# Sorting the tokens of three batches by expert: 48 dense expert tiles become 19 gathered ones

## The chip, the cores and the metric

The kernel runs on one core of one Trainium2 chip, in one launch; the other cores do nothing. The metric is the device time of one execution in microseconds (us). Engines are named as in the profile: PE (TensorE, with PEld for its weight loads), DVE (VectorE), ACT (ScalarE), POOL (GpSimd) and SP (SyncE, which here mostly issues DMAs). A letter q behind an engine's name means the sequencer of that engine, with waits and DMA issues.

## The reference, cut to what matters

A decoder of two layers works on x of 4 batches x 256 tokens x 256 features, all in float32. Layer 0 has self-attention, attention over a memory of 4 x 1601 x 256, and a quantised feed-forward. Layer 1 has a recurrence, a cross attention (16 query heads of 128 features, 4 key/value heads, 256 + 1601 = 1857 keys, taken in 15 chunks of 128), and then, last, a mixture of eight experts of which each token uses two:

```python
xf = layernorm(x).reshape(-1, 256)                # 1024 tokens
top_logits, top_idx = top_k(xf @ w_gate, 2)       # 8 experts
weights = softmax(top_logits)
# for each token, over its two experts e:
h0, h1 = xf @ wi_0[e], xf @ wi_1[e]               # 256 -> 128 each
y = (silu(h0) * h1) @ wo[e]                       # 128 -> 256
out = x + sum over the two of weight * y
```

The reference sorts the 2048 (token, expert) pairs by expert and multiplies each group by its expert's weights; any way that gives the same sum will do.

## The kernel before, in words

One function, `decoder_kernel`, holds the program. Its parts are Python generators: each `yield` ends a piece, and the order in which pieces are called is the order in which work reaches the scheduler. The scheduler fixes the order on every engine when the kernel is built; on the chip each engine then works through its own list strictly in order, and waits at an instruction until its inputs and buffers are ready. SP issues nearly all DMAs, also in order.

In the first part four generators `before(b)`, one for each batch, run staggered up to the recurrence of layer 1. In the second part `steps()` walks through the cross attention. Its unit is a `Pair`: one batch, one key/value head and two query heads (b, g, h), 32 pairs in all, each with eight steps of two key chunks. A pair's number is in its tile names (`sum320` is the sum of pair b=3, g=2, h=0). For each step

- `score` multiplies keys by queries (L1361, tile `bsc`); ACT copies the scores out into an `s` tile of a ring of twelve (L1362), DVE keeps a running maximum (L1364, L1366),
- `exponential` follows ten steps later: DVE subtracts the maximum (L1383), ACT takes the exponential (L1386), POOL adds the two chunks to the pair's `sum` (L1389, L1398),
- `weigh` follows eleven steps later: the `s` tiles times the values (L1407, tile `bpo`); `finish` turns the sum (L1421), and multiplies by the output weights (L1437, tile `bpw`), which DVE adds to `x` (L1441).

Each step has two places, 2s and 2s+1, at which `others(place)` runs small pieces of other work. `put(place, gen, last, bank)` books them: the keys and queries of the next head (`prep_kv`, `prep_q`, with their rotation on DVE and POOL and the product `pk` at L1290), the pieces of `maximum` and `finish`, and the experts of batches 0, 1 and 2, which can start when their batch's attention is over.

`experts(b)` is dense: all eight experts are worked out for all 256 tokens, and the gates are zero where a token did not choose the expert. It normalises x (`mo`), multiplies by the gate weights (`pl`), finds the two largest of eight by comparisons on DVE, and then for each expert

- `inner(e)`: four matmuls of 128x256 into `mph` (L1053), one tanh on ACT (L1058), two DVE operations of 128x256 (L1059, L1060);
- `outer(e, it)`: two matmuls of 128x256 into `mpe` (L1066), two DVE operations x += gate * y (L1071).

Three batches x eight experts x two halves of the tokens are 48 expert tiles of 128 rows. The pieces of batches 0 and 1 are all placed between attention steps; of batch 2 the last six pieces (`KEPT = 3`, two at a time) are left until the last attention is over, where they run with the first pieces of `experts(3)`. After that `experts(3)` ends the kernel.

Of the kernel before, what the change touches and what calls it, by code (L numbers as in the profile page):

```python
# [10 lines left out]
F32 = mybir.dt.float32  # L11
I32 = mybir.dt.int32
# [3 lines left out]
AF = mybir.ActivationFunctionType  # L16
ALU = mybir.AluOpType
AX = mybir.AxisListType
# [16 lines left out]
TERN = 34  # L35
SIDE = 48
KEPT = 3
KEYS = (3,)
EARLY = tuple((b, i) for b in range(3) for i in range(4))
LATE = tuple((3, i) for i in range(4))  # L40
# [4 lines left out]
RATE = 1  # L45
START = (0, 3, 8, 13)
NE, ME = 8, 128
NEG = -1.0e30
SCALE1 = float(np.float32(1.0) / np.sqrt(HD1).astype(np.float32))
QCLIP = 128.0 - 1e-6  # L50
# [6 lines left out]
def _constants():  # L57
    f = np.float32
    p = np.arange(P)
    c = {}  # L60
    c["ident"] = np.eye(P, dtype=f)

    c["tri"] = np.where(p[None, :] <= p[:, None], 0.0, NEG).astype(f)

    c["par"] = (p[:, None] // HD0 % 2 == np.arange(2)[None, :]).astype(f)

    def interleaved(ang):
        cos, sin = np.cos(ang.astype(np.float64)), np.sin(ang.astype(np.float64))
        return np.repeat(cos, 2, 1), np.stack([-sin, sin], -1).reshape(len(ang), -1)

    def halves(ang):
        cos, sin = np.cos(ang.astype(np.float64)), np.sin(ang.astype(np.float64))
        return np.concatenate([cos, cos], 1), np.concatenate([-sin, sin], 1)

    t = np.arange(S, dtype=f)[:, None]
    freq0 = (np.arange(0, HD0, 2, dtype=f) / f(HD0)) * np.log(f(30000.0))
    freq1 = f(1.0) / f(10000.0) ** (np.arange(0, 16, 2, dtype=f) / f(16))
    for n, (cc, ss) in (("r0", interleaved(t * freq0[None])), ("r1", halves(t * freq1[None]))):
        for m, a in (("c", cc), ("s", ss)):
            c[n + m] = a.astype(f).reshape(2, P, 16).transpose(1, 0, 2).reshape(P, 32)  # L80
    c["ones"] = np.ones((P, P), f)
    freq2 = 1.0 / 10000.0 ** (np.arange(0, HD1, 2) / HD1)
    c["invf"] = np.broadcast_to(freq2.astype(f)[None], (P, 64))
    ch = p // 32
    same = ch[:, None] == ch[None, :]
    c["cum"] = (same & (p[:, None] <= p[None, :])).astype(f)
    c["first"] = (same & (p[:, None] % 32 == 0)).astype(f)
    last = p % 32 == 31
    k8 = np.arange(8)
    selc = [(last[:, None] & (4 * j + ch[:, None] <= k8[None])) for j in range(2)]  # L90
    sell = [(last[:, None] & (4 * j + ch[:, None] == k8[None])) for j in range(2)]
    c["selcum"] = np.stack(selc, 1).astype(f).reshape(P, 16)
    c["sellast"] = np.stack(sell, 1).astype(f).reshape(P, 16)
    c["selstab"] = np.broadcast_to((p == 31)[:, None], (P, 8)).astype(f)
    sx = np.zeros((P, 8), f)
    sx[:8] = k8[:, None] < k8[None]
    c["strict8"] = sx
    ex = np.zeros((P, 2, P), f)
    for j in range(2):
        ex[:8, j] = k8[:, None] == 4 * j + ch[None]  # L100
    c["expand"] = ex.reshape(P, 2 * P)
    c["dmask"] = (p[:, None] % 16 == np.arange(16)[None]).astype(f)
    c["iota8"] = np.broadcast_to((k8 - 8.0)[None], (P, 8)).astype(f)
    at, off = {}, 0
    for n, a in c.items():
        at[n] = (off, a.shape[1])
        off += a.shape[1]
    return np.ascontiguousarray(np.concatenate(list(c.values()), 1), dtype=f), at
# [8 lines left out]
def decoder_kernel(ctx: ExitStack, tc: tile.TileContext, at, t, out):  # L117
# [43 lines left out]
    def fa(b, name, dt=F32):  # L161

        return fr.tile([P, 512], dt, tag=f"a{b}", name=name, bufs=NA)
# [5 lines left out]
    def db(name):  # L169

        return wk.tile([P, 1024], F32, tag="db", name=name, bufs=NDB)

    def sm(shape, tag, name, bufs=2, dt=F32):
        return small.tile(shape, dt, tag=tag, name=name, bufs=bufs)
# [34 lines left out]
    def cc(name):  # L209
        o, n = at[name]  # L210
        return cst[:, o : o + n]
# [83 lines left out]
    def centred(xh, xb, mv, r):  # L295
        xh = xh.rearrange("p (j d) -> p j d", j=2)
        nm = sm([P, 2], "nmr", f"nmr{uid()}", 4)
        V.scalar_tensor_tensor(nm, mv[:, :, 0], -1.0, r[:, 0:2], ALU.mult, ALU.mult)
        for j in range(2):
            A.activation(xh[:, j, :], xb[:, j, :], AF.Identity, bias=nm[:, j : j + 1], scale=r[:, j : j + 1])  # L300
        return xh
# [674 lines left out]
        yield  # L976


    def experts(b):
        xb = xs[b]  # L980

        final = b == B - 1

        def ea(name, place=0):
            return fa(place if final else 2, name)

        wgt = sm([P, 2, NE], "wgt", f"wgt{b}", 1)
        nc.sync.dma_start(out=wgt, in_=t["wgt"].rearrange("(c p) n -> p c n", p=P))
        s8 = [P, 2, NE]
# [3 lines left out]
        r1 = rsqrt(mv[:, :, 1], 1e-5, f"mo{b}")  # L993
        yield
        xh = centred(ea(f"mxh{b}"), xb, mv, r1)
        yield
        tp = to_features(xh, f"mo{b}")
        yT = ea(f"yTm{b}")
# [12 lines left out]
        for k in range(2):  # L1011
            m = sm([P, 2], f"m{k}", f"mm{b}{k}", 1)
            V.tensor_reduce(m, lg, AX.X, ALU.max)
            oh = sm(s8, f"oh{k}", f"oh{b}{k}", 1)
            V.tensor_tensor(oh, lg, m[:, :, None].to_broadcast(s8), ALU.is_equal)
            V.tensor_mul(oh, oh, iota)
            ix = sm([P, 2], "ix", f"ix{b}{k}", 1)
            V.tensor_reduce(ix, oh, AX.X, ALU.min)
            V.tensor_tensor(oh, iota, ix[:, :, None].to_broadcast(s8), ALU.is_equal)
            if k == 0:  # L1020
                V.scalar_tensor_tensor(lg, oh, NEG, lg, ALU.mult, ALU.add)
            tops.append(m)
            hots.append(oh)
# [4 lines left out]
        w1 = sm([P, 2], "w1", f"w1{b}", 1)  # L1028
        V.tensor_scalar(w1, w2, 1.0, None, ALU.add)
        V.reciprocal(w1, w1)  # L1030
        V.tensor_scalar(w1, w1, 0.5, None, ALU.mult)
        V.tensor_mul(w2, w2, w1)
        gts = sm(s8, f"gts{final}", f"gts{b}", 1)
        V.tensor_mul(gts, hots[0], w1[:, :, None].to_broadcast(s8))
        V.tensor_mul(hots[1], hots[1], w2[:, :, None].to_broadcast(s8))
        V.tensor_add(gts, gts, hots[1])
        yield
        weights = {}

        def inner(e):  # L1040
            e2 = e - e % 2
            if e == e2:
                wi = db(f"wi{b}{e2}").rearrange("p (i c n) -> p i c n", i=2, c=2)
                for i, name in enumerate(("wi0", "wi1")):
                    nc.sync.dma_start(
                        out=wi[:, i], in_=t[name][:, e2 * ME : (e2 + 2) * ME].rearrange("(c p) n -> p c n", p=P)
                    )
                weights[e2] = wi, weight(fa(3, f"we{b}{e2}"), "woe", e2 * ME, (e2 + 2) * ME, 0, D)
            wi = weights[e2][0]
            ph = p1(f"mph{b}{e}")  # L1050
            for i in range(2):
                for c in range(2):
                    T.matmul(  # L1053
                        ph[:, i * 256 : i * 256 + 256], lhsT=wi[:, i, c, e % 2 * ME : (e % 2 + 1) * ME], rhs=yT[:, c, :],
                        start=c == 0, stop=c == 1,
                    )
            it = ea(f"it{b}{e}", 1)[:, 0:256]
            A.activation(it, ph[:, 0:256], AF.Tanh, scale=0.5)  # L1058
            V.scalar_tensor_tensor(it, it, 1.0, ph[:, 0:256], ALU.add, ALU.mult)  # L1059
            V.tensor_mul(it, it, ph[:, 256:512])  # L1060
            return it
# [11 lines left out]
                )  # L1073


        ahead = 2 if final else 0
        its = []
        for e in range(NE + ahead):
            if e < NE:
                its.append(inner(e))  # L1080
                if not final:
                    yield
            if e >= ahead:
                outer(e - ahead, its[e - ahead])
            yield
        for j in range(2):
            (nc.scalar if final and j else nc.sync).dma_start(out=out[b, j * P : (j + 1) * P], in_=xb[:, j, :])
        yield

    def before(b):  # L1090
# [15 lines left out]
    def run(gen):  # L1106
        for _ in gen:
            pass
# [351 lines left out]
    def put(place, gen, last=False, bank=False):  # L1460
        while bank and place in taken:
            place += 1
        if bank:
            taken.add(place)
        places.setdefault(place, []).append((gen, last))
        return place
# [46 lines left out]
        gen = loader(b, g)  # L1513
        put(base + 60, gen, True)
    for b in range(B - 1):
        gen = experts(b)
        spot = 2 * (64 * (b + 1) + 17)

        pieces = 23 if b < B - 2 else 23 - 2 * KEPT
        for i in range(pieces):  # L1520
            spot = put(spot, gen, i == 22, i not in (0, 1, 2, 5, 6)) + (5 if i > 6 else 3)
    kept = gen

    def others(place):
        for gen, last in places.pop(place, ()):
# [72 lines left out]
    gen = experts(B - 1)  # L1598
    for _ in range(KEPT):
        next(gen)  # L1600
        next(kept)
        next(kept)
    run(kept)
    run(gen)


# [63 lines left out]
```

## Time and profile before

| what | value |
|---|---|
| median of three runs | 1749.77 us (1748.74 to 1751.0) |
| the profiled execution | 1749.43 us, of which 1747.4 us is the span in the trace |
| mean granted TensorE clock | 0.993 |
| engine with the largest share of the span | PE, 97% |
| end of the last attention matmul (`bpw`, L1437) | 1712.0 us |
| from there to the span's end | 35.4 us |

In the answers of the trace a line of the timeline reads: start in us, busy us, engine, line, operation, output <- inputs, shapes, number of instructions run together, and in brackets the idle time ahead of it and what ended that. A float32 matmul leaves two matmul records, so eight records of `mph` are the four matmuls of one expert. Busy times of a row of matmuls overlap a little; the distance from one start to the next row's start is the time that the work takes of the engine's order. "PEclk" is the clock that the chip granted to TensorE, 1 being full.

### The profile page before, as it was taken

How to read it: one execution, taken by the hardware profiler on the slowest of the kernel's cores; microseconds unless marked ns; L12 is line 12 of the kernel's file. 1: busy time of each engine (PE TensorE's matmuls, PEld its weight loads, DVE VectorE, ACT ScalarE, POOL GpSimd, SP SyncE). 2: the span in 40 equal slices, each digit the busy share in tenths (PEclk: the TensorE clock that was granted, in tenths of full speed). 3: DMA queues.
4: the chain of work that ended last, by engine and by line, in shares of the span. 5: the costliest groups of instructions: out<-in, count | busy, mean ns of one | idle time of the engine just before them, and what ended most of it. 6: DMA issues, size and time to landing. Idle time of an engine off the chain costs nothing.

```text
span 1747.4 us, 20643 instructions
## 1 busy us (share of the span) xinstructions
PE 1694.9 (97%) x6642; PEld 971.5 (56%) x6642; DVE 1302.7 (75%) x2429; ACT 997.4 (57%) x1742; POOL 877.5 (50%) x719
## 2 busy tenths in 40 slices
PE   8899989999999999999999999999999999999998
PEld 4455668765555455554555555555555555445546
DVE  6653476787668777787877878777877878788776
ACT  3456653656456656566665656556565656656551
POOL 2210032211126576676766756655665776676651
PEclk9999999999999999999999999999999999999999
DMA  7221334212231121121212121121222113011102
GB/s 258 99 90 50 90 99 128 75 66 90 97 109 46 38 82 35 55 58 31 89 32 70 47 67 52 55 82 35 73 61 67 51 37 93 26 37 48 43 0 67
DMA packets 113554, 119.10 MB, mean 68 GB/s; under 512 B 10000, under 2 KB 87332, under 8 KB 113448
## 3 DMA queue, kind: packets, MB, share of 16 engines
q1 hardware_dynamic: 111624, 116.39, 21.6%
q10 hardware_dynamic: 1824, 1.41, 0.3%
q8 instruction: 53, 0.87, 0.2%
q14 instruction: 53, 0.43, 0.1%
HBM read 100.20 MB, written 17.57 MB: 67 GB/s over the span
## 4 chain that ended last, share of the span: by engine, by line
PE 64%; DVE 12%; POOL 9%; ACT 9%; issue 4%; DMA 1%; POOLq 0%; DVEq 0%; ACTq 0%
PE bpo L1407 17%; PE bsc L1361 16%; PE pk L1290 5%; POOL sum L1398 5%; PE mph L1053 2%; PE bpw L1437 2%; PE vah L355 2%; ACT s L1386 2%; ACT s L1362 2%; DVE acc L1366 1%; PE xpo L740 1%; DVE s L1383 1%; PE pq L1239 1%; POOL ropeq L1196 1%; PE xsc L695 1%
## 5 line engine op out<-in xcount | busy, mean ns | idle before, releaser
L1398 POOL TENSOR_TENSOR sum<-sum,s 128x512 f32<-128x512 f32 (+1 forms) x411 | 536.7, 1306 | 84.1 <-ACT s L1386 59.0
L1361 PE MATMUL bsc<-qTb,kTb 128*128 128x512 f32 (+1 forms) x960 | 459.5, 599 | 6.8 <-ACT kTb L1303 6.7
L1407 PE MATMUL bpo<-s,vb 128*128 128x512 f32 (+1 forms) x960 | 459.9, 598 | 0.4 <-ACT s L1386 0.4
L1362 ACT ACTIVATE s<-bsc,kn 128x512 f32<-128x512 f32 (+1 forms) x480 | 316.5, 683 | 211.6 <-PE bsc L1361 194.6
L1366 DVE SCALAR_TENSOR_TENSOR acc<-bsc,kn,acc 128x512 f32<-128x512 f32 x448 | 333.0, 743 | 89.2 <-ACT s L1362 73.3
L1383 DVE TENSOR_TENSOR s<-s,bc 128x1024 f32<-128x1024 f32 (+1 forms) x256 | 289.4, 1142 | 14.7 <-PE bc L1379 14.5
L1386 ACT ACTIVATE s<-s 128x1024 f32<-128x1024 f32 (+1 forms) x256 | 256.5, 1006 | 53.8 <-DVE s L1383 52.2
L1361 PEld LDWEIGHTS bsc<-qTb,kTb 128*128 128x128 f32 (+1 forms) x960 | 174.2, 188 | 191.9 <-issue 135.3
L1407 PEld LDWEIGHTS bpo<-s,vb 128*128 128x128 f32 (+1 forms) x960 | 169.8, 191 | 141.7 <-issue 137.9
L1389 POOL TENSOR_TENSOR sum<-s 128x512 f32<-128x512 f32 x32 | 40.8, 1276 | 198.6 <-ACT s L1386 198.6
L1196 POOL TENSOR_TENSOR ropek<-ropek,ropuk 128x512 f32<-128x512 f32 (+1 forms) x64 | 78.2, 1222 | 123.7 <-DVE ropuk L1191 122.4
L1203 ACT ACTIVATE ropeq<-ropeq,rnq 128x128 f32<-128x128 f32 x128 | 41.2, 390 | 110.7 <-POOL rnq L1199 107.1
L355 PE MATMUL vah<-wv,vcT 128*128 128x512 f32 (+1 forms) x156 | 77.7, 633 | 5.1 <-DMA vcT<-in_ctxT 3.1
L1290 PEld LDWEIGHTS pk<-wkv,cTk 128*128 128x128 f32 x624 | 76.3, 192 | 8.3 <-issue 4.5
L1290 PE MATMUL pk<-wkv,cTk 128*128 128x128 f32 x624 | 77.4, 275 | 0.0
L1199 POOL TENSOR_TENSOR kn<-ssk,nhalf 128x4 f32<-128x4 f32 (+1 forms) x64 | 66.2, 1034 | 17.5 <-DVE ssk L1198 15.0
L1364 DVE TENSOR_SCALAR acc<-bsc,kn 128x512 f32<-128x512 f32 x32 | 24.0, 750 | 59.7 <-ACT s L1362 59.7
L1437 PEld LDWEIGHTS bpw<-wo,aT 128*128 128x128 f32 x256 | 48.5, 190 | 34.8 <-issue 21.1
L272 POOL TENSOR_TENSOR rsr_xa<-rse_xa,nhalf 128x2 f32<-128x2 f32 x4 | 3.4, 854 | 126.0 <-DVE rse_xa L270 126.0
L1437 PE MATMUL bpw<-wo,aT 128*128 128x256 f32 x256 | 65.6, 379 | 0.3 <-ACT aT L1413 0.3
L1196 POOL TENSOR_TENSOR ropeq<-ropeq,ropuq 128x512 f32<-128x512 f32 x32 | 43.8, 1368 | 40.2 <-PE bsc L1361 17.8
L358 ACT COPY vst<-vah 128x512 f32<-128x512 f32 (+1 forms) x52 | 30.2, 591 | 56.0 <-issue 18.3
(509 smaller groups left out, 2589.7 us busy)
## 6 DMA issues: line engine op xcount, KB each, us to landing
v<-vst SPq DMA_DIRECT2D x48, 256.0 KB
vb<-v SPq DMA_DIRECT2D x48, 256.0 KB
cTk<-in_ctxT SPq DMA_DIRECT2D x24, 512.0 KB
wq<-in_wq SPq DMA_DIRECT2D x16, 512.0 KB
wo<-in_wo SPq DMA_DIRECT2D x16, 512.0 KB
wi<-in_wi SPq DMA_DIRECT2D x32, 256.0 KB
xcT<-in_ctxT SPq DMA_DIRECT2D x12, 512.0 KB
xct<-in_ctx SPq DMA_DIRECT2D x12, 512.0 KB
```

The costliest lines, as they stand in the source:

```text
L355: T.matmul(pv[0:r, :], lhsT=cT[:, c, k * P : k * P + r], rhs=wv[c], start=c == 0, stop=c == 1)
L1196: G.tensor_tensor(r4, r4, u4[:, :, ::-1, :], ALU.add)
L1199: G.tensor_tensor(rn, ss[:, 0:n], nhalf[:, 0:n], ALU.pow)
L1290: T.matmul(pk[:, q, 0:w], lhsT=src, rhs=e["wkv"][:, c, 0:w], start=c == 0, stop=c == 1)
L1361: T.matmul(pc[0:n, :], lhsT=e["kT"][:, k * P : k * P + n], rhs=q, start=True, stop=True)
L1362: A.activation(s[0:n, i, :], pc[0:n, :], AF.Copy, scale=e["kn"][0:n, k : k + 1])
L1366: V.scalar_tensor_tensor(self.acc[0:n, :], pc[0:n, :], e["kn"][0:n, k : k + 1], self.acc[0:n, :], ALU.mult, ALU.max)
L1383: V.tensor_tensor(s[0:n, 0:w, :], s[0:n, 0:w, :], self.bc[0:n, None, :].to_broadcast([n, w, 512]), ALU.subtract)
L1386: A.activation(s[0:n, 0:w, :], s[0:n, 0:w, :], AF.Exp)
L1398: G.tensor_tensor(self.sum[0:n, :], self.sum[0:n, :], s[0:n, i, :], ALU.add)
L1407: T.matmul(self.po, lhsT=e["v"][0:n, k, :], rhs=self.s[c][0:n, i, :], start=k == 0, stop=k == NCH - 1)
L1437: T.matmul(pw[:, j * 256 : j * 256 + 256], lhsT=aT[:, o : o + P], rhs=e["wo"][:, self.h + h, :], start=True, stop=True)
```

## The change

For batches 0, 1 and 2 the dense experts go; `experts(3)` stays as it was. In their place:

- `chosen(b)` holds the normalisation, the gates and the choice as before. `places_of(b)` runs it, and keeps the one-hot choices (12 columns of 128 choices: 3 batches x 2 choices x 2 halves), counts per expert, each choice's rank among the equal choices (two small matmuls), the norms and the two gate values.
- `clear(b)` writes zeros over a DRAM buffer `rows_in` of 19 x 128 rows of 1 KB (one POOL memset and three to four SP DMAs in each of two batches, six in all).
- `slots()` then works out, when batch 2's choice is known, how many tiles of 128 rows each expert needs (never over 19 in all), the slot of each of the 1536 choices, and the expert of each tile, an integer `ei`.
- Twelve indirect DMAs issued by POOL (128 rows of 1 KB each, each row to the address in its own slot number) scatter the normalised rows to `rows_in`.
- Ten turns take two tiles each (the last takes one). `fetch` loads two tiles of rows and, for each, reads the tile's expert into a register of SP and loads that expert's `wi0`, `wi1` and `wo` from an address made of the register. `turn` transposes the rows (four transposes, one ACT copy of 128x512). `inside` has eight matmuls of 128x128 (the work of two tiles), one tanh, two DVE operations of 128x256. `outside` has two matmuls of 128x256, one ACT copy, and an SP DMA to a second DRAM buffer, `rows_out`.
- At the end twelve indirect DMAs on POOL gather each token's two rows from `rows_out`, twelve DVE operations of 128x256 add them to x by their gate values, and six DMAs write the output.

Seven preparing pieces and 21 pieces of the turns are booked at free places behind batch 2's choice, between attention steps; the rest (the last turns and the gathers) is called after the attention, in alternation with the pieces of `experts(3)`.

The core of the diff:

```diff
 NE, ME = 8, 128
+NSLOT = 19
...
+    rows_in = dram.tile([NSLOT * P, D], F32, tag="rin", name="rows_in")
+    rows_out = dram.tile([NSLOT * P, D], F32, tag="rout", name="rows_out")
...
+        for b in range(B - 1):
+            xh = fa(2, f"sx{b}").rearrange("p (j d) -> p j d", j=2)
+            for j in range(2):
+                A.activation(
+                    xh[:, j, :], xs[b][:, j, :], AF.Identity, bias=norms[:, b, 2 + j : 3 + j], scale=norms[:, b, j : j + 1]
+                )
+            for k in range(2):
+                for j in range(2):
+                    c = 4 * b + 2 * k + j
+                    G.indirect_dma_start(
+                        out=rows_in[:, :], out_offset=bass.IndirectOffsetOnAxis(ap=slot[:, c : c + 1], axis=0),
+                        in_=xh[:, j, :], in_offset=None,
+                    )
+            yield
...
+        def fetch(i):
+            m = min(2, NSLOT - i)
+            xr = fa(2, f"xr{i}").rearrange("p (n d) -> p n d", d=D)
+            nc.sync.dma_start(
+                out=xr[:, 0:m, :], in_=rows_in[i * P : (i + m) * P, :].rearrange("(n p) d -> p n d", p=P)
+            )
...
+            for q in range(m):
+                e = nc.sync.value_load(ei[0:1, i + q : i + q + 1], min_val=0, max_val=(NE - 1) * ME)
+                for k, name in enumerate(("wi0", "wi1")):
+                    nc.sync.dma_start(
+                        out=wi[:, q, k], in_=t[name][:, bass.ds(e, ME)].rearrange("(c p) n -> p c n", p=P)
+                    )
+                nc.sync.dma_start(out=wo[:, q, :], in_=t["woe"][bass.ds(e, ME), :])
...
+        todo = list(range(0, NSLOT, 2))
+        fetch(todo[0])
+        yield
+        turn(todo[0])
+        fetch(todo[1])
+        yield
+        for n, i in enumerate(todo):
+            inside(i)
+            yield
+            if n + 1 < len(todo):
+                turn(todo[n + 1])
+                yield
+            outside(i)
+            if n + 2 < len(todo):
+                fetch(todo[n + 2])
+            yield
+        for b in range(B - 1):
+            for j in range(2):
+                g = fa(2, f"sg{b}{j}")
+                for k in range(2):
+                    c = 4 * b + 2 * k + j
+                    G.indirect_dma_start(
+                        out=g[:, k * D : (k + 1) * D], out_offset=None, in_=rows_out[:, :],
+                        in_offset=bass.IndirectOffsetOnAxis(ap=slot[:, c : c + 1], axis=0),
+                    )
+                for k in range(2):
+                    c = 4 * b + 2 * k + j
+                    V.scalar_tensor_tensor(
+                        xs[b][:, j, :], g[:, k * D : (k + 1) * D], share[:, c : c + 1], xs[b][:, j, :], ALU.mult, ALU.add
+                    )
+                nc.sync.dma_start(out=out[b, j * P : (j + 1) * P], in_=xs[b][:, j, :])
+                yield
...
     for b in range(B - 1):
-        gen = experts(b)
+        gen = places_of(b)
...
+    kept = slots()
+    for i in range(7):
+        spot = put(spot, kept, False, i < 2) + 3
+    for i in range(SLOTTED):
+        spot = put(spot, kept, False, True) + 3
...
     gen = experts(B - 1)
     for _ in range(KEPT):
         next(gen)
-        next(kept)
-        next(kept)
-    run(kept)
+        for _ in range(2):
+            next(kept, None)
+    for _ in kept:
+        next(gen, None)
     run(gen)
```

## The prediction, made before the changed kernel ran

> **What bounds the kernel now.** I read the page's shares and its chain first, then the windows of the second part, then timelines of PE and POOL around the places where the change books its pieces.
>
> ```profile
> span 1747.4 us, 20643 instructions
> PE 1694.9 (97%) x6642; PEld 971.5 (56%) x6642; DVE 1302.7 (75%) x2429; ACT 997.4 (57%) x1742; POOL 877.5 (50%) x719
> ...
> PE 64%; DVE 12%; POOL 9%; ACT 9%; issue 4%; DMA 1%; POOLq 0%; DVEq 0%; ACTq 0%
> ```
>
> PE carries the end: it is busy for 97% of the span. The same holds where the dense experts lie (920 to 1580; columns: stretch, its length, then busy us of PE, PEld, DVE, ACT, POOL, clock, DMA):
>
> ```profile
> 920.00:1580.00 660.00, 647.25 (x2300) 354.34 (x2299) 530.18 (x875) 391.66 (x653) 432.52 (x347) 0.99 0.19 56
> ```
>
> PE has 98%, DVE 80%, POOL 66%. So matmul time that is removed here should shorten the span, and a wait put into PE's order lengthens it. The prices of matmul work come from PE's timeline, start to next start:
>
> ```profile
> 917.91 1.95 PE L1290 MATMUL pk<-wkv,cTk 128*128 128x128 f32 x16
> 919.70 1.88 PE L1407 MATMUL bpo<-s,vb 128*128 128x512 f32 x4
> ...
> 924.00 1.89 PE L1053 MATMUL mph<-yTm,wi 128*128 128x256 f32 x8
> 925.72 1.88 PE L1407 MATMUL bpo<-s,vb 128*128 128x512 f32 x4
> ...
> 932.66 0.60 PE L1301 MATMUL tpk<-cst,ropek 128*128 128x128 f32 x4
> 933.10 1.02 PE L1407 MATMUL bpo<-s,vb 128*128 128x512 f32 x2
> ...
> 937.06 1.03 PE L1066 MATMUL mpe<-we,it 128*128 128x256 f32 x4
> 937.92 1.88 PE L1361 MATMUL bsc<-qTb,kTb 128*128 128x512 f32 x4
> ```
>
> One dense expert costs PE 1.73 + 0.86 = 2.59 us. One sparse turn of two tiles is four transposes, 0.43 (the `tpk` row), eight matmuls of 128x128, 1.79 (the `pk` row, 16 records), and two of 128x256, 0.86 (the `mpe` row): 3.08 us.
>
> **1. Matmul work before the last attention's end E (1712.0).** Of the 24 dense experts 21 start before E (168 of the 256 `mph` records): 21 x 2.59 = 54.4 us go. In the changed kernel's order of instructions six turns are finished before E, 6 x 3.08 = 18.5, and parts of two more, 0.43 + 1.79 + 0.43 = 2.65; the ranking matmuls are 16 records of at most 0.1 us (eight `pl` records take 0.8), 1.6. Net -31.7 us. The slot count is fixed at 19, so no draw of the tokens alters this.
>
> **2. The scatters, a new wait.** Each of the twelve scatters writes the same buffer `rows_in`, and in the order as built each waits until the one before has landed; the first row load waits for the twelfth. That order puts them on POOL behind the first add of chunk 5 of `sum312`, with sixteen ordinary POOL operations between them. The first transposes of gathered rows (`stp0`) stand on PE right behind the first of `bpw312`'s matmuls, and PE, in order, holds everything behind them: scores, values, later turns.
>
> ```profile
> 1574.76 12.08 POOL L1398 TENSOR_TENSOR sum<-sum,s 128x512 f32<-128x512 f32 x9 [2.40 <-ACT s L1386]
> 1587.73 1.27 POOL L1196 TENSOR_TENSOR ropeq<-ropeq,ropuq 128x512 f32<-128x512 f32 x1 [0.90 <-DVE ropuq L1191]
> 1588.96 1.23 POOL L1199 TENSOR_TENSOR rnq<-ssq,nhalf 128x4 f32<-128x4 f32 x1
> ...
> 1600.66 1.27 POOL L1389 TENSOR_TENSOR sum<-s 128x512 f32<-128x512 f32 x1 [4.54 <-ACT s L1386]
> ```
> ```profile
> 1613.99 1.88 PE L1407 MATMUL bpo<-s,vb 128*128 128x512 f32 x4
> 1615.70 1.03 PE L1437 MATMUL bpw<-wo,aT 128*128 128x256 f32 x4
> ```
>
> The fifth of the nine adds ends at 1574.76 + 5 x 1.34 = 1581.5. On this clock (attention as before up to here) PE reaches `stp0` at 1616.1, less the 3.45 us of dense experts that lay between 1581.5 and there: 1612.7. Let i be POOL's time for a scatter, L the time until it has landed, F the load of `xr0`. Three of the gaps between scatters hold three or four ordinary operations, 4.0 + 4.0 + 5.2 us, more than L; the nine others, the last landing among them, cost L. The last scatter has landed at 1581.5 + 13.2 + 12i + 9L; the stall is 12i + 9L + F - 18.
>
> No indirect DMA is in the trace of before. Bounds: i between the smallest and the largest POOL rows, 0.70 and 2.35; L between 1.2 (the longest that SP ever waited for an output DMA) and 2.5 (the last output DMA: issue over at 1744.86, span's end 1747.4).
>
> ```profile
> L726 POOL TENSOR_TENSOR xacc<-xacc,xs 128x1024 f32<-128x1024 f32 x4 | 9.4, 2352 | 5.6 <-ACT xs L722 5.5
> L272 POOL TENSOR_TENSOR rsr_mo<-rse_mo,nhalf 128x2 f32<-128x2 f32 x4 | 2.8, 704 | 6.5 <-DVE rse_mo L270 6.4
> ```
> ```profile
> 1744.50 0.36 ACTq L1087 DMA_DIRECT2D out<-x  x1
> ```
>
> I take i = 1.3, the common POOL row of 128 partitions (L1398: 1.3), because a scatter handles 128 rows too; L = 2.5, since the row that it is nearest to is the same kind of 128 KB write to DRAM, and F = 2.5 likewise. Stall: 15.6 + 22.5 + 2.5 - 18 = 22.6 us. POOL falls behind by less than that and catches up while PE waits; ACT and DVE, blocked by the ring of twelve `s` tiles, show the same stall a little earlier and add nothing.
>
> The Trainium skill has two rules on i and L. "DMA: Bandwidth & Descriptors", section "Anatomy of one DMA — SWDGE (gpsimd) path", fits about 2.0 us + bytes / 436e3 for a whole DMA issued by GpSimd, 2.3 us at 128 KB; with i = 1.0 and L = 1.3 the sum would be about -14 us (1736), an estimate. Against the change speaks "SBUF — State Buffer", section "SBUF: two separate sides": GpSimd can't write descriptors while DVE holds their shared port, and the DMA starves; no run here shows it, and POOL's adds of 1.3 us reach at most 2.6 beside a busy DVE.
>
> **3. The clock after a stall.** After 2.34 us without matmuls, the trace shows two pairs of scores in 3.07 instead of 1.88 us, with the granted clock at 0.50:
>
> ```profile
> 1549.72 0.66 PE L1373 MATMUL tm<-cst,acc 128*128 128x128 f32 x4 [2.34 <-DVE acc L1366]
> ...
> 1551.57 3.07 PE L1361 MATMUL bsc<-qTb,kTb 128*128 128x512 f32 x4
> ```
>
> One such restart after the stall: +2 us (0 if there is none).
>
> **4. The tail.** Before, E to the span's end is 35.4 us: three dense experts of batch 2, the gate chain of batch 3 until 1722, eight experts. After E the order as built has the remaining turns between the gate chain's steps; PE's work up to `spe18`, the last of them, is 0.86 x 2 + 1.79 x 2 + 0.22 + 0.43 + 0.86 + 0.9 + 0.8 + 1.72 + 0.43 = 10.7, with 1.8 us of waits like those of before (1.38 us for DVE): E + 12.5. Copy 0.4, issue 0.4, landing 2.5: rows complete at E + 15.8. Only then do the twelve gathers run, on POOL one behind another without waits for each other: the last lands 12i + L = 18.1 later, E + 33.9. DVE's order puts all gather adds ahead of the third expert's `x +=`, so that six experts' adds (12 x 0.47) and four experts' products (4 x 0.84), 9.1 us, and an output DMA of 2.9 come behind: E + 45.9, against 35.4: +10.5 us. PE is idle there; its experts are not the bound.
>
> **5. Loads and small work.** SP's 19 register reads and the loads behind them (four DMA issues of 0.38 us for a pair) stand ahead of keys and values of head 3 of batch 3; fifteen reads in a row, between 0.36 each (SP's issue row) and 1.3 (a POOL row; no read is in this trace), near the first as it is SP's own, and some 13 issues are 5 to 20 + 5 us, hidden in the scatter chain's 50; what is not hidden, with the refilling of the pipeline, costs by my estimate 2 us (0 to 8). The ACT copies (0.4 to 0.7 each, ACT at 59%), the zeroing DMAs and the ranking on DVE (less than the 21 x 1.79 us of expert operations that leave DVE) lie beside PE's work: nothing. Without that cover the 1.6 us of ACT and DVE work of a turn would be exposed ten times.
>
> **The sum.** -31.7 + 22.6 + 2 + 10.5 + 2 = +5.4 us: 1749.4 + 5.4 = 1754.8 for the profiled run, and by the median of before, 1749.77, 1755. As a formula: change = 24i + 10L - 50.8. It breaks even at i = 1.08 with L = 2.5.
>
> **The rivals.** *Cheap scatters* (the other sign): i = 1.0, L = 2.0, stall 14.5 and gathers done at E + 29.8; -6.8 us, 1743. It decides from 24i + 10L below 50.8. For it: a scatter has no arithmetic over 512 columns as the adds have. Against it: POOL's 128x4 row, though tiny, takes 1.03 us too, and a write must land before the next. At both lowest bounds: -22, 1728. *Dear scatters*: i = 2.35, L = 2.5: +30.6, 1780. For it: the addresses are worked out row by row; against it only that few rows on POOL are so long. *DVE as second bound*: DVE is busy for 80% where sixteen dense experts lie; if the steps can shrink only by DVE's share there, 16 x 1.79 = 28.7 instead of PE's 41.4, 12.7 us are lost: 1768. For it: 12% of the chain is DVE; against it: PE's 98% there and no row of waits on DVE long enough.
>
> **How the numbers follow.** Forecast 0.40, cheap scatters 0.33, DVE 0.12, dear scatters 0.15. The forecast's own range is 1745 to 1765 (L or i off by a fifth). The range 1730 to 1782 takes in the price bounds of i and L nearly whole, leaving out 2 in 10 at both ends. A measurement of this kernel can tell 0.2%, 3.5 us, from no change. Slower by more: the DVE and dear cases and most of the forecast, 0.50. Faster by more: the cheap case and a little of the forecast, 0.37. Within: 0.13.
>
> **What would show it.** Right: twelve POOL DMAs in a chain near 1555 to 1605 with a landing wait after most; one PE idle of some 20 us ending at `stp0` released by the load of `xr0`; PE busy about 30 us less in total; the tail near 46 us with DVE waiting for gathers. Wrong: no idle ahead of `stp0` (the sum would be about -19), scatters above 2 us, idle of PE in many small pieces at `sph` or `stp` (weights or rows loaded late, step 5), or DVE busier than 90% in the steps before.

## The result and the profile after

The changed kernel takes 1761.7 us (median of four, 1760.6 to 1766.5) against 1749.3 of the kernel before on the same chip: slower by 12.5 us. The ratio on record is 1.0083, with a 95% interval of 1.0069 to 1.0098 (the two medians alone give 1.0071). 1755 was forecast, with a range of 1730 to 1782. The profiled execution is the slowest of the four, and 2.3 us of its excess are there already at the first score maximum of the attention, ahead of anything that the change moves.

```profile
span 1764.7 us, 20865 instructions
PE 1681.1 (95%) x6598; PEld 954.3 (54%) x6598; DVE 1280.6 (73%) x2400; ACT 1001.4 (57%) x1754; POOL 904.2 (51%) x745
```

PE is busy for 14 us less where 31.7 us of work (net) were taken out ahead of E, and idle for longer. The mean granted clock is 0.982, against 0.993. The last attention matmul ends at E = 1717.4 (1712.0 before), and 47.3 us of tail follow (35.4 before). So of 17.3 us in the profiled execution 5.4 arise before E and 11.9 behind it.

PE's timeline has the places (idle time ahead in brackets, and what ended it):

```profile
1457.31 1.11 PE L1573 MATMUL bc<-cst,mq 128*128 128x128 f32 x4 [5.99 <-DVE mq L1569]
...
1551.86 2.73 PE L1555 MATMUL bsc<-qTb,kTb 128*128 128x512 f32 x4 [2.51 <-ACT kTb L1497]
1574.28 1.12 PE L1573 MATMUL bc<-cst,mq 128*128 128x128 f32 x4 [4.14 <-DVE mq L1569]
...
1592.76 0.59 PE L1631 MATMUL bpw<-wo,aT 128*128 128x256 f32 x2
1604.10 1.11 PE L1162 MATMUL stp<-cst,xr 128*128 128x128 f32 x4 [10.74 <-DMA xr<-rows_in]
```

The predicted stall at the first gathered tile is there, half as long as forecast; 4.1, 2.5 and 6.0 us of idle ahead of it were not forecast (of the 2.5 us the kernel before has a like, 2.34 us at 1549). Where the two long ones come from is to be read from the other engines. First 1571, all engines in order of time:

```profile
1563.39 1.52 POOL L1132 DMA_INDIRECT rows_in<-sx,cst  x1 [0.41 <-DMA rows_in<-sx,cst]
...
1567.72 0.96 POOL L1132 DMA_INDIRECT rows_in<-sx,cst  x1 [2.80 <-DMA rows_in<-sx,cst]
...
1568.70 1.27 POOL L1390 TENSOR_TENSOR ropeq<-ropeq,ropuq 128x512 f32<-128x512 f32 x1
1569.92 1.04 POOL L1393 TENSOR_TENSOR rnq<-ssq,nhalf 128x4 f32<-128x4 f32 x1
1570.99 1.28 ACT L1397 ACTIVATE ropeq<-ropeq,rnq 128x128 f32<-128x128 f32 x4 [8.54 <-POOL rnq L1393]
...
1572.88 0.75 DVE L1558 TENSOR_SCALAR acc<-bsc,kn 128x512 f32<-128x512 f32 x1 [8.82 <-ACT s L1556]
1573.54 0.68 DVE L1569 TENSOR_REDUCE mq<-tm 128x4 f32<-128x512 f32 x1
```

Four engines hang on one chain: scatters stand on POOL ahead of `ropeq` and `rnq`; ACT waits for `rnq` for 8.5 us with its score copies behind; DVE waits for the copies for 8.8 us with the maximum `mq` behind; PE waits for `mq`. At 1451 the same shape has another head, batch 2's normalisation:

```profile
1446.26 5.28 POOL L1592 TENSOR_TENSOR sum<-sum,s 128x512 f32<-128x512 f32 x4
...
1453.28 0.70 POOL L275 TENSOR_TENSOR rsr_mo<-rse_mo,nhalf 128x2 f32<-128x2 f32 x1
1454.01 0.16 DVE L301 SCALAR_TENSOR_TENSOR nmr<-mv_mo,rsr_mo 128x2 f32<-128x2 f32 x1 [8.24 <-POOL rsr_mo L275]
```

`nmr` waits on DVE for POOL's power, which stands behind four sums and two operations on keys; the kernel before had the same two instructions with a wait of 1.9 us. After each of the six gaps of 2.25 us and more between 1300 and E, PE restarts slowly; here the one at 1574, in windows (stretch, length, busy us of PE, PEld, DVE, ACT, POOL, the granted clock, DMA share and GB/s):

```profile
1574.00:1576.00 2.00, 1.72 (x5) 1.25 (x6) 2.00 (x5) 0.57 (x1) 0.85 (x1) 0.50 0.19 66
1576.00:1578.00 2.00, 2.00 (x4) 0.92 (x3) 1.90 (x4) 0.69 (x1) 1.61 (x2) 0.50 0.00 0
1578.00:1580.00 2.00, 2.00 (x3) 0.66 (x3) 2.00 (x3) 1.24 (x2) 0.64 (x1) 0.50 0.19 66
1580.00:1582.00 2.00, 2.00 (x8) 1.01 (x7) 2.00 (x3) 1.90 (x4) 1.64 (x2) 0.93 0.08 21
```

Busy time x (1 - clock) is the loss: 0.86 + 1.0 + 1.0 + 0.14 = 3.0 us here. Summed in the same way it is 1.7 at 1351, 1.75 at 1457, 1.7 at 1522, 1.7 at 1552 and 1.7 at 1604: 11.5 us between 1300 and E, where the kernel before has one of 1.7 at 1551.

The prices of the new operations, in the group of the scatters, and the tail:

```profile
L1132 POOL DMA_INDIRECT rows_in<-sx,cst x12: 960/986/1524, 1555.3 to 1598.8; - x12
...
DMA to landing us min/median/max: 2.4/2.4/4.1
```
```profile
1735.71 1.04 POOL L1218 DMA_INDIRECT sg<-rows_out,cst  x1 [15.58 <-ACT it L1254]
...
1750.09 0.95 POOL L1218 DMA_INDIRECT sg<-rows_out,cst  x1 [0.30 <-issue]
...
1752.95 0.48 DVE L1224 SCALAR_TENSOR_TENSOR x<-sg,cst,x 128x256 f32<-128x256 f32 x1 [0.28 <-DMA sg<-rows_out,cst]
```

A scatter takes POOL 0.99 us and has landed 2.4 us after its start (medians); gathers follow each other at 1.3 us, the last addition comes at E + 35.6, and 11.8 us of the last batch's experts and of output follow.

### The profile page after: what moved, and what is told of

Same layout as the page of the kernel before. It is cut to its first block, busy times and chain, and to the rows that moved or that the text cites. A ratio compares the mean times of both kernels' runs of the same rounds, so it can differ in the third digit from the quotient of the medians.

```text
span 1764.7 us, 20865 instructions
## 1 busy us (share of the span) xinstructions
PE 1681.1 (95%) x6598; PEld 954.3 (54%) x6598; DVE 1280.6 (73%) x2400; ACT 1001.4 (57%) x1754; POOL 904.2 (51%) x745
## 5 line engine op out<-in xcount | busy, mean ns | idle before, releaser
L1555 PE MATMUL bsc<-qTb,kTb 128*128 128x512 f32 (+1 forms) x960 | 464.2, 604 | 12.1 <-ACT kTb L1497 12.0
```

Source lines behind the costliest of these rows:

```text
L1555: T.matmul(pc[0:n, :], lhsT=e["kT"][:, k * P : k * P + n], rhs=q, start=True, stop=True)
```

## The experiments

Positions are compared at the start of the transposes `tm`, of which each of the 32 pairs has one: "at tm29" is the difference there to the kernel before. E and the tail are read as above. All these come from profiled executions, and that of the changed kernel is its slowest. Where no number of runs is given, there was one; the kernel before took 1747.5 to 1749.8 us (medians) on the chips of these runs, so a difference in time of some 3 us to the changed kernel tells nothing by itself. Comments in the diffs are added for the text.

**Is matmul time really what bounds?** The kernel before without the experts of batches 0 to 2:

```diff
-    for b in range(B - 1):
+    for b in range(0):
         gen = experts(b)
...
-    kept = gen
+    kept = iter(())
```

> The kernel before, with the experts of batches 0, 1 and 2 left out altogether (normalisation, choice, dense experts). It measures what 62.2 us of removed expert matmuls (plus some 5 of gates and transposes) are worth, with no sorting in the way. Theory (POOL and the engines behind it become the bound where the matmuls were cover): 10 to 20 us of it are not gained: 1697 to 1707, with new PE waits for maxima and keys. Rival (PE alone is the bound): 1749 less 62 to 67, 1682 to 1688.

1693.0 us; E = 1655.7, tail 35.3. PE's waits from 500 on stay small ones:

```profile
PE bsc L1361 <- ACT kTb L1303: 11.2, 15, 1.2
PE bc L1379 <- DVE mq L1375: 7.0, 3, 2.5
```

My theory here fell, and the rival's 1682 to 1688 was not reached either. At tm31 56.0 us are gained, where 54.4 us of expert matmuls and a little of gates and transposes are gone: no second bound on DVE or POOL. The total gains 55 of the 62 because the tail's three dense experts had lain beside the last batch's gate chain, which now makes PE wait (3.7 us) and then costs it 4.3 us at half the clock. Up to tm25 the changed kernel is within 3.8 us of this run (-32.8 against -36.6), a difference of the size of its gates and ranking. So its losses are not a general price of less cover: but for the restart at 1351, which this run has too, they come from 1446 on.

**What do the scatters cost?** Scatters left out:

```diff
-                    G.indirect_dma_start(
-                        out=rows_in[:, :], out_offset=bass.IndirectOffsetOnAxis(ap=slot[:, c : c + 1], axis=0),
-                        in_=xh[:, j, :], in_offset=None,
-                    )
+                    pass
```

> The twelve scatters are left out, and the row loads read the zeroed buffer. Theory (scatters cost the 10.7 us at the first gathered tile, most of the 4.1 us at the maximum and three half-clock restarts of some 1.7 us): 16 to 20 us less than 1762, so 1742 to 1746, with the 6.0 us wait for the maximum near 1457 still there. Rival (the wait moves on to something else, such as the weight loads by register): idle of 5 us or more at the first tiles' matmuls, and 1752 or more.

1743.8 us, as expected, 17.9 below the changed kernel's median; at tm29 -29.5 against -7.2: by the profiled executions the scatters cost 22.3 us in that stretch. The 6.0 us wait at 1457 remains, and so does the one for `kTb` at 1552 (2.9 us here), whose origin stays open; no wait above 0.2 us appears at a gathered tile ahead of E, and the tail is unchanged (46.9).

**Is it the landing waits?** One buffer for each scatter:

```diff
-                        out=rows_in[:, :], out_offset=...
+                        out=apart[c][:, :], out_offset=...
```

> Each scatter writes a DRAM buffer of its own, so none waits for the one before; the row loads read the last buffer alone (eleven twelfths of the rows are left out). Theory (the landing waits between scatters make the stall): POOL's idle of 8.2 us between scatters goes, the last scatter ends about 8 us earlier, PE's idle ahead of the first gathered tile falls from 10.7 to under 3 us, the wait of 4.1 us for the maximum shrinks, and one or two restarts at half clock go: the time falls by 10 to 14 us from 1762, to 1748 to 1752. Rival (POOL's own 1.0 us for each scatter and its sums make the lateness): the idle stays above 7 us and the time falls by less than 4 us.

1757.4 us, and -15.5 at tm29: of the 22.3 us 8.3 are saved, and some 4 of these are half clock that did not come, 1.7 of them behind a gap of 2.26 us at 1521 that the changed kernel has too. Neither side was right. The stall at the first tile is gone, but without the chain the scheduler puts the scatters together, with three sums between them, ahead of `ropeq`, and a wait as long as the stall stands at the maximum instead:

```profile
1571.40 0.96 POOL L1133 DMA_INDIRECT rows_in<-sx,cst  x1 [0.30 <-issue]
...
1573.61 1.26 POOL L1391 TENSOR_TENSOR ropeq<-ropeq,ropuq 128x512 f32<-128x512 f32 x1
```
```profile
1579.19 1.11 PE L1574 MATMUL bc<-cst,mq 128*128 128x128 f32 x4 [11.53 <-DVE mq L1570]
```

The place on POOL costs, chained or not.

**POOL relieved.** Half of the sums left out:

```diff
-                for i in range(w):
+                for i in range(1):
                     G.tensor_tensor(self.sum[0:n, :], self.sum[0:n, :], s[0:n, i, :], ALU.add)
```

> POOL adds only one of the two chunks of each attention step but the first (the softmax sums are incomplete), which takes some 220 adds of 1.3 us off POOL. Theory (POOL is the second bound: without the dense matmuls PE runs ahead of it): the 6.0 us wait near 1457 falls below 3 us, and the waits for keys and maxima on PE together fall from 29 to about 15 us; the scatters start earlier too, the idle at the first gathered tile falls below 5 us; 1740 to 1748. Rival (DVE is the second bound): those waits stay within 4 us of 29, and the time falls by less than 6 us.

1722.0 us, more gained than expected: PE's waits for keys and maxima fall from 29.1 to 6.6 us, and the wait near 1457 is gone; the idle at the first gathered tile is not (10.4 us). The run doesn't separate causes well: it gains 7 us by tm8 already, where the kernel before is the same program, so less work on POOL helps the attention by itself, change or no change.

**The wait at batch 2's normalisation.** `nmr` held behind what is in DVE's list already, and five places later:

```diff
-        gen = places_of(b)
+        gen = orderly(places_of(b), (2,))     # piece 2 keeps behind what was issued before it
...
-... + (2 if i in (2, 4, 5, 6) else 3)
+... + (2 if i in (2, 4, 5, 6) else 8 if i == 1 else 3)
```

> One piece is moved: the step of batch 2's normalisation that waits on DVE for POOL's power (nmr) is put behind what is already in DVE's list, some five places later; the same for batches 0 and 1. Theory (DVE, in order, holds the maximum behind nmr while POOL works off its sums): the 6.0 us wait near 1457 and its restart at half clock of 1.7 us go: 6 to 8 us less than 1762, 1754 to 1756. Rival (POOL is late there in any case, and PE meets it at the next maximum or key): less than 3 us.

The wait and its restart go: -33.9 at tm26 against -26.7, 7.2 us as expected, and at E 8.8. The total is 1758.4, only 3.3 below the median of the changed kernel. By the profiled executions it is 8.1 (spans of 1756.6 and 1764.7); a single run can't say how much of that the median would keep.

**The tail.** First, additions called later:

```diff
-                g = fa(2, f"sg{b}{j}")
+                g = fb(1 + (2 * b + j) % 3, f"sg{b}{j}")[:, 0:512]
...
-    for _ in kept:
-        next(gen, None)
+    for _ in range(3):
+        next(kept)
+        next(gen)
+    for _ in range(6):
+        next(gen)
+    for _ in kept:
+        next(gen, None)
```

> Only the order at the end is changed: the gathered rows go to other buffers, and their additions are called behind most of the last batch's experts. Theory (the gathers delay the last batch's experts, which stand behind them on DVE): the end is the last gather (about 36 us behind the last attention matmul) plus 0.5 + 0.4 + 2.9: 39 to 41 us of tail in place of 47.5, 1753 to 1756 in all. Rival (DVE's own work sets the tail): less than 3 us.

1757.9 us (four runs), ratio 1.0066 (1.0048 to 1.0084) to the kernel before; the tail is 44.5, 2.8 us less, not 39 to 41. The order as built still had the first additions ahead of the second expert's, since the scheduler takes the call order only as a wish. With the additions held behind (the dependency that the kernel's own `behind` adds), and all gathers in one piece ahead of them:

```diff
+HOLD = 12
...
+    next(kept)                      # the twelve gathers
+    for _ in range(HOLD - done):    # pieces of experts(3), to its third expert
+        next(gen)
+    for _ in range(6):
+        behind(kept)                # two additions
+        next(gen, None)
```

> Only the end of the changed kernel is reordered, more strictly than in the run with late additions, where the order as built still had the first additions ahead of the second expert's: all gathers are issued at once into buffers of their own, and the additions of each pair are held behind the third, fourth ... eighth expert of the last batch on DVE. Theory (the tail is set by the gathers' landing, once no expert waits for them): last landing at E + 36, tail 40 to 42 us in place of 47.5: 1753 to 1756. Rival (DVE's own work sets the tail): 1758 to 1762.

1756.1 us, tail 40.0, the length that the theory gave: 7.3 of the 11.9 us by which the tail had grown were the order on DVE. Its sentence on what then sets the tail does not hold, though. No addition waits for a gather any more, and DVE is busy for 12.73 of the last 13.1 us of additions (columns as in the windows above), so here the rest is DVE's own work, as the rival said (its 1758 to 1762 was missed):

```profile
1738.50:1751.60 13.10, 9.71 (x44) 7.89 (x42) 12.73 (x31) 1.15 (x3) 5.92 (x6) 0.99 0.45 136
```

**The scatters apart.** Each scatter a piece of its own, held behind POOL's list, three places apart:

```diff
-            for k in range(2):
-                for j in range(2):
+                for k in range(2):          # inside the loop over j
                     c = 4 * b + 2 * k + j
                     G.indirect_dma_start(...)
-            yield
+                    yield
...
-    kept = slots()
-    for i in range(7):
+    kept = orderly(slots(), range(3, 15))
+    for i in range(3):
         spot = put(spot, kept, False, i < 2) + 3
...
+    for i in range(12):
+        spot = put(spot, kept) + 3
+    spot = put(spot, kept) + 8
```

> The twelve scatters become twelve pieces, three places apart and each behind what is already in POOL's list; the two ACT copies of a batch are apart as well; the first turn follows the last scatter, so that some six turns in place of four lie behind the attention. Still one buffer, each scatter waiting for the one before. Theory (the scatters cost 22 us by standing close together on POOL ahead of ropeq and rnq, with ACT and DVE waiting behind): no PE idle above 3 us between 1540 and 1610, E some 30 us earlier, the tail 8 to 11 us longer for the moved turns: 1740 to 1744. Rival (a turn in the tail is set by SP's eight loads of it, 4 us and more, and not by matmuls): 1749 or more.

1766.2 us. The trace shows both a gain and a loss. Between 1550 and 1620 no PE idle above 0.8 us but one of 2.6 and one of 1.8 is left, and E is 24.8 us earlier (1692.6), though some 9 of these are three turns' matmuls moved behind E (88 of the 152 `sph` records are left there, 40 in the changed kernel). But the tail is 71.8 instead of 47.3: the end calls the turns in alternation with the last batch's experts, and the last turn is done only at 1739.82:

```profile
1715.49 6.03 PE L1248 MATMUL mph<-yTm,wi 128*128 128x256 f32 x16 [4.65 <-DMA wi<-in_wi]
...
1739.82 0.59 PE L1188 MATMUL spe<-swo,sit 128*128 128x256 f32 x2
```

By then the experts are nearly over, so that the twelve gathers lie behind them and not beside them. I had reckoned with 8 to 11 us. Loads, the rival, have a share: a wait of 4.65 us for an expert's weights is PE's longest in this tail; how much of the 24.5 us it makes was not separated.

**All three together**: the three diffs above, and an end that calls the turns first:

```diff
+    for i in range(46 - booked[0]):     # turn pieces left behind the attention
+        next(kept)
+        if i % 2 and done < 6:          # beside the gate chain of experts(3)
+            next(gen)
+            done += 1
```

> The three together: scatters spread, nmr behind, additions behind the experts. If the causes are separate their gains add up (20 + 7 + 6 us): 1727 to 1735, faster than the kernel before by 0.7 to 1.2%. If they are the same wait seen at several places, 1742 or more.

1738.4 us (six runs), ratio 0.9949 (0.9929 to 0.9969): faster than both kernels. E = 1681.3 (again with three turns moved behind it), tail 54.0, with no PE idle above 2.6 us from 1430 on, and a mean clock of 0.993. Less than hoped for: in the tail a turn takes 4.1 to 5.2 us where its matmuls are 3.1, two of them waiting for rows (0.3 and 0.6 us), and `wi` is 1.1 us late for the first dense expert.

**Two batches sorted, the third dense.**

```diff
-NSLOT = 19
+NSLOT = 15
+NB = 2
...
-    for b in range(B - 1):
+    for b in range(NB):
         gen = places_of(b)
...
+    kept = experts(2)
+    spot = 2 * (64 * 3 + 17)
+    for i in range(23 - 2 * KEPT):
+        spot = put(spot, kept, False, i not in (0, 1, 2, 5, 6)) + (5 if i > 6 else 3)
```

> Only batches 0 and 1 are sorted, into 15 tiles; batch 2 stays dense as in the kernel before. The scatters are over some 30 us before their first use and the gathers lie between attention steps. Matmul work: 32 dense tiles of 1.3 us (41.4) become 15 of 1.54 (23.1) and about 1 us of ranking, -17. Theory (the loss was in the stall at the first tile, in the tail, and in waits on POOL): no stall above 3 us at a gathered tile, the tail within 1 us of the 35.4 of before, and of the 17 us 5 to 10 lost to waits: 1737 to 1744, faster than both. Rival (twenty more POOL operations and the register loads cost more wherever they lie): 1750 or more.

A clear miss: 1757.1 us (five runs), ratio 1.0056 (1.0037 to 1.0075). The gain at tm19 (-21.1) is lost by tm27 (+3.4). Matmuls explain 1 of these 24.5 us (20.7 us of turns and 1 of ranking stand in this stretch against the 20.7 of batch 1's dense experts); the rest went mostly in waits of PE (14.2 us, 5.0 before) and half clock behind them (9.0 us). One of the waits, at 1488, runs through POOL, ACT and the keys:

```profile
1485.25 1.03 POOL L1399 TENSOR_TENSOR rnq<-ssq,nhalf 128x4 f32<-128x4 f32 x1
1486.31 0.69 ACT L1403 ACTIVATE ropeq<-ropeq,rnq 128x128 f32<-128x128 f32 x2 [3.92 <-POOL rnq L1399]
...
1487.48 0.57 ACT L1503 COPY kTb<-tpk 128x512 f32<-128x512 f32 x1
...
1488.10 3.78 PE L1561 MATMUL bsc<-qTb,kTb 128*128 128x512 f32 x4 [3.49 <-ACT kTb L1503]
```

No indirect DMA stands on POOL near it: the scatters were over at 1285, the gathers start at 1559.

The same plan with scatters and gathers as single pieces, `nmr` held behind, the first turn after them:

```diff
+    kept = orderly(slots(), list(range(3, 11)) + list(range(36, 50)))
+    for i in range(11):
+        spot = put(spot, kept, False, i < 2) + 3
+    spot += WAIT                    # 4 in place of 14
```

> Two sorted batches again, now with the steps that helped with three: scatters and gathers as single pieces some places apart, nmr behind what is already in DVE's list, the first turn later. If the waits of the run with two batches (3.2 and 2.4 us at the scatters near 1260, 3.9, 3.5, 1.9 and 2.9 us later, and the half clock after them) came from POOL operations bunched ahead of rnq and nmr, they go, and the matmul balance of -17 us shows: 1736 to 1742. If they come from the turns themselves (their ACT copies, loads and places between the attention's steps), 1750 or more again.

1735.5 us (four runs), ratio 0.9920 (0.9903 to 0.9937), the lowest of the kernels that do all the work, though its interval meets that of the three together: waits for keys fall from 21.3 to 12.6 us. All the moves together are worth these 21.6 us; which of the moved pieces did how much was not separated, so that bunching was the cause is not shown, and why the gain still falls from 25.1 us at tm22 to 13.8 at tm27 was not traced.

## Why the prediction was right in sign, and where its steps failed

**The matmul work (step 1)** held. The run without experts shows it to be worth its full time, so the rival of DVE as a second bound is out.

**The scatters (step 2)** came out near in sum and wrong in make-up. For a scatter i was 0.99 us, not 1.3; L was 2.4 - 0.99 = 1.4 us, not 2.5. My formula with these gives 12 + 12.6 + 2.5 - 18 = 9.1 us at the first tile, and 10.7 were there, but two errors cancel in that agreement:

```profile
1548.42 6.69 POOL L1592 TENSOR_TENSOR sum<-sum,s 128x512 f32<-128x512 f32 x5 [4.53 <-ACT s L1580]
...
1598.79 0.99 POOL L1132 DMA_INDIRECT rows_in<-sx,cst  x1 [0.15 <-issue]
```

From the end of the fifth add (1555.1) to the last landing (1598.8 + 2.4 = 1601.2) the chain took 46.1 us. The formula gives 51.3 with my prices and 37.8 with the measured ones. Not most but five of the scatters waited for a landing, 8.2 us in all; two of them were held until 1.9 and 1.5 us after the median landing, POOL waited 1.4 us for DVE ahead of `ropek`, and in one gap the two ordinary operations outlasted L by 1.0. PE for its part came to `stp0` 38.3 us after the add (1592.8 + 0.6 = 1593.4) and not 31.2, held up by the unforeseen idle and the half clock. So of the 11.9 us by which the stall was too long in the forecast, the chain makes 5.2 and PE's lateness 7.0 (the load took 0.4 more). What failed is the sentence that ACT and DVE "show the same stall a little earlier and add nothing". They brought 4.1 us of idle and the restarts, and the whole cost 22.3 us, close to the 24.6 of steps 2 and 3 by luck. In the tail, i of the gathers from start to start was 1.31, as forecast; even so the measured prices, 12 x 0.99 + 12 x 1.31 + 9 x 1.4 + 2.1 = 42, lie below the formula's 50.8, on the side of the cheap rival, which said 1743 and a faster kernel. The sign came out right through what the formula left out. (The lower bound of 0.70 us was also misread: memsets and casts on POOL took 0.1 to 0.3 in the kernel before. The measured i lies inside either way.)

**The clock (step 3)** was five times its forecast: one restart of 2 us was expected, and 11.5 - 1.7 = 9.8 us were lost. I priced the restart rightly (1.7 us) and counted one, where gaps of 2.25 us and more came six times, one of them as before.

**The tail (step 4)** held: +11.9 where +10.5 was forecast, first gather at E + 18.3 (15.8), last addition at E + 35.6 (33.9), the rest 11.8 us (12.0). The run with additions in order confirms its reason for 7.3 of the 11.9 us.

**Step 5** counted the ranking and the normalisation on DVE as work beside PE's: nothing. Work was the wrong measure; `nmr` is 0.16 us long, and its wait in DVE's list cost 6.0 us and a restart. The 2 us for loads were not there: ahead of E no wait of PE ended with a weight load.

The account of the profiled execution up to E closes nearly: -31.7 of work, +23.6 of PE waits from 1000 on (35.8 against 12.2), +9.8 of clock, +2.3 from the start: +4.0, against 5.4 measured. Beside the forecast, the stall is 11.9 us too long, 12.9 us of waits stand in no step, and the clock is 7.8 short: the total came within 7 us because these errors have two signs.

Two rules of the Trainium skill were weighed. "DMA: Bandwidth & Descriptors" (section "Anatomy of one DMA — SWDGE (gpsimd) path") fits 2.0 us + bytes / 436e3 to a DMA issued by GpSimd, by my estimate 2.3 us for 128 KB: the scatters' 2.4 from start to landing (median) agree, while the gathers took 2.8 to 4.2. "SBUF — State Buffer" (section "SBUF: two separate sides") warns that GpSimd can't write descriptors while DVE runs an operation in a mode that locks the port they share. Which of DVE's operations here run in such a mode was not looked at; most scatters took 0.96 to 1.0 us beside a DVE at work, the longest 1.5 (1.8 with twelve buffers), so no long starvation shows in these traces.

## What to carry to other kernels

An operation that is put on a helper engine costs what stands behind it there: look up in the order as built which instruction on that engine another engine's next step needs, and keep long or chained operations apart from it. Count idle gaps, not only idle time: in these runs most of those of 2.25 us and more were followed by half the clock for 3 to 6 us, and those of 2.15 us and less in the attention were not. When matmuls are taken out or moved across the end of the main loop, plan the tail anew; the transfers that used to lie beside work can end up behind it.

## What the runs showed of the hardware

An indirect DMA of 128 rows of 1 KB held POOL for 0.94 to 1.0 us in most cases (the longest 1.8); with nothing between them one started 1.26 us after the other, and it landed 2.4 (scatter) or 3.1 us (gather) after its start, by the medians of the changed kernel. Gaps of about 2.5 us on PE were followed by half the granted clock in some executions (2.53 us, then four records of `bsc` in 3.42 us, with twelve buffers) and not in others (2.51 us, then 1.98 us, with `nmr` behind); what decides between the two is left open.
